# Routed experts of a decoder layer: the next block's transposes stand ahead of the up product, and streamed weights land in 14 places instead of 10

## The chip, the cores and the metric

The kernel runs on one core of one Trainium2 chip. The metric is the device time of one execution in microseconds, as the median of several runs. Besides, one execution was profiled by the hardware; durations of single instructions come from that one.

## The reference

One decoder layer works on 4096 tokens (2 sequences of 2048) of width 512, in float32. Three parts follow each other, each added to its input: an attention whose keys and values are fixed weights, with squared ReLU in place of the softmax; a cross-attention of 16 heads onto 128 context rows; and a mixture of experts. The last part is what the change is about, cut to its core:

```
shared = (silu(x @ sg) * (x @ su)) @ sd                  # every token, inner width 1024
e      = argmax(x @ gate_w);  xs = x * sigmoid(max(x @ gate_w))
for each expert r of 32, on the tokens with e == r:
    h      = silu(xs @ rg[r]) * (xs @ ru[r])              # 512 -> 1024
    routed = h @ rd[r]                                    # 1024 -> 512
out = x_in + shared + routed
```

Each expert has three matrices of 2 MB (gate, up, down), so the 32 experts read 201 MB of weights once.

## The kernel before, in words

TensorE works in float32r, a rounded format, so every float32 operand is split into a high part (a rounding copy) and a low part (the difference). A product takes three matmuls, low x high, high x low and high x high (`three`, L162). The high part is made by ScalarE (L93) and the low part by VectorE or POOL (L96), in `split`. In the profile the parts are named with h and l at the end: rh and rl of weights, th and tl of transposed inputs, hh and hl of hidden values.

The stages are `stage0` (attention), `stage1` (cross-attention, and the router's logits), `shared` with the first 768 of the shared expert's 1024 inner columns, and `routed`, which holds the experts and the last 256 inner columns of the shared expert (class `Rest`, L798). An `overflow` loop at the end takes tokens that didn't fit; here it runs no turn.

**The routed stage.** Experts are ranked by their number of tokens, and each rank has a fixed capacity (L30): 448, 384, five of 256, four of 192, thirteen of 128, eight of 64. A capacity is cut into blocks of 256, 128 or 64 rows. The order (L862 to L869, L1023 to L1033) mixes them: a large expert, then one of 64, then one of 128, and after each expert that isn't of 128 a block of the rest (256 tokens of the shared expert's remainder), until the sixteen of those are used. So a typical round is 256, rest, 64, rest, 128; the last rounds are 192 (128 + 64), 128, 128 without any rest.

The loop over the blocks (L1079 to L1100) is a pipeline written out by hand. For block i it emits:
- `prepare` (L1036) of block i+2: the indirect gather of its rows on POOL's queue (L905), or the rest's four z loads on SyncE's queue (L812),
- `load` of the next expert's gate weights, if this is the expert's last block,
- `first`: the gate product of block i (L941 for up to 128 rows; L986, with half of gate and up together, for 256; L823 for the rest),
- `load` of the next expert's up weights,
- `turn_hidden` of block i-1: its hidden values are transposed by TensorE (L912, `ht`) and split into th and tl,
- `second`: the up product of block i, after which VectorE or POOL multiplies it into the gate's silu,
- `turn_x` of block i+1: its gathered rows are transposed by TensorE (L912 or L931, `pt`) and split,
- `third`: the down product of block i-1 (L941, L1011 or L852), the copy out of PSUM (L1017, L855), and POOL's transfer that adds it into the output (L1019, L856),
- `load` of the next expert's down weights.

**Weights.** `load` (L882) takes eight pieces of 128 x 512 (256 KB) of one matrix. Each lands by SyncE's queue (L893) in a raw place, is cast by ScalarE into rh and gets its rl from VectorE; then the place is free. There are ten raw places: six of the pool `raw` (L55) and four of the tag F (L48). L872 says in which order they are taken. The split pieces of gate and up lie in a pool W of 48, of which the rest's weights hold some; those of down in the tags A and B, eight each.

**Other places.** Transposed inputs have two places each for th (tag J) and tl (tag K). A block of up to 128 rows takes one of each, a block of 256 both. Gathered rows have three (H). [...] P1 for the down product and for `pt` of up to 128 rows, P2 for gate, P3 for up, P4 for `ht` and for `pt` of 256 rows. The tag F serves earlier stages too: a low part in `stage0` and `stage1`, and the second half of the input tiles z of every other turn of `shared`.

**What sets the order.** The loop gives the instructions priorities in the order of emission. When the program is built, a scheduler places them on each engine's queue, by those priorities and its own estimate of when operands are ready; so casts of weights and casts of inputs are interleaved on ScalarE. On the chip each queue runs in that fixed order. An instruction that waits holds all that stand behind it on its engine.

## Time and profile before

| | us |
|---|---|
| median of 3 runs | 2779.28 (2778.81 to 2779.35) |
| the profiled execution | 2778.45 |
| its span, first to last instruction | 2776.4 |
| granted TensorE clock over the span | 0.993 of full speed |

| stretch of the span, us | what runs | TensorE busy | DMA, GB/s |
|---|---|---|---|
| 800 to 1000 | cross-attention | 195.81 of 200 | 69 |
| 1600 to 1700 | shared expert | 100.00 of 100 | 85 |
| 2000 to 2100 | routed experts | 98.11 of 100 | 275 |
| 2600 to 2700 | routed experts, last rounds | 96.46 of 100 | 305 |

How to read the lines that follow: the first number of a timeline line is the start in us from the span's begin, the second the time in us; then come the engine, the line of the kernel, the operation, and output <- inputs. In brackets stands how long the engine had been idle and what ended that. A busy share of TensorE counts overlapping matmuls, and the end of a matmul is modelled: a 512-column matmul is shown with 0.39 us, but in an unbroken row one starts every 0.227 us. In a table of stretches the columns are the stretch, its length, the busy us of TensorE, its weight loads, VectorE, ScalarE and POOL (with numbers of instructions), the granted TensorE clock, the busy share of the DMA engines and GB/s.

### The profile page before, as it was taken

Reading aid. Unit: us, or ns where it says so; the run is one execution under the profiler, and the core shown is the slowest. Engines: PE = TensorE matmul, PEld = TensorE weight load, DVE = VectorE, ACT = ScalarE, POOL = GpSimd, SP = SyncE. Lnnn points to the kernel's source line nnn. Section 1 sums busy time; section 2 is a strip of 40 time slices with the busy share of each in tenths; the row PEclk is TensorE's granted clock in tenths of the full one; section 3 lists DMA queues with packets and bytes.
Section 4 is the critical chain, followed back from the end, with each engine's and each line's share of the span. In section 5 each row is a group of like instructions: output and inputs, shape, how many; then the busy total and the mean of one; then the engine's idle time right before and its main releaser. Section 6 shows DMA issues by size and latency. Waiting matters only on the chain. (4 is left out here: it accounts for less than half of the span.)

```text
span 2776.4 us, 47492 instructions
## 1 busy us (share of the span) xinstructions
PE 2694.0 (97%) x14788; PEld 2298.8 (83%) x14788; DVE 2054.5 (74%) x4671; ACT 1793.1 (65%) x3995; POOL 1023.1 (37%) x821
## 2 busy tenths in 40 slices
PE   7999999999999999999999999999999999999997
PEld 5877877777878999899988888888888988877876
DVE  8888888889887988888878522245677777777885
ACT  6787777787867777777774111135566666667774
POOL 5686566677643333333330120002122222223232
PEclk9999999999999999999999999999999999999999
DMA  4022212212120223222245322255798989988984
GB/s 139 31 69 73 73 54 77 72 50 76 36 81 25 86 78 115 86 93 74 81 155 183 103 92 87 91 175 165 250 284 269 285 257 292 280 276 254 307 300 144
DMA packets 238001, 396.70 MB, mean 143 GB/s; under 512 B 29377, under 2 KB 67281, under 8 KB 237745
## 3 DMA queue, kind: packets, MB, share of 16 engines
q1 hardware_dynamic: 223024, 366.45, 39.2%
q0 software_dynamic: 14720, 27.19, 5.1%
q8 instruction: 117, 1.92, 0.3%
q14 instruction: 140, 1.14, 0.1%
HBM read 311.67 MB, written 83.83 MB: 142 GB/s over the span
## 5 line engine op out<-in xcount | busy, mean ns | idle before, releaser
L96 DVE TENSOR_TENSOR rl<-raw,rh 128x512 fp32r<-128x512 f32 x768 | 512.1, 711 | 124.1 <-ACT rh L93 116.6
L93 ACT CAST rh<-raw 128x512 fp32r<-128x512 f32 x768 | 446.3, 621 | 146.3 <-DMA raw<-in_rg 85.1
L96 POOL TENSOR_TENSOR pl<-p,ph 128x512 fp32r<-128x512 f32 x320 | 427.9, 1346 | 243.2 <-ACT ph L93 217.7
L343 DVE TENSOR_TENSOR p<-s,rl 128x512 f32<-128x512 f32 x512 | 343.2, 683 | 80.7 <-ACT rl L341 60.4
L93 ACT CAST ph<-p 128x512 fp32r<-128x512 f32 x448 | 277.3, 622 | 153.9 <-DVE p L343 148.4
L341 ACT ACTIVATE rl<-s 128x512 f32<-128x512 f32 x512 | 301.5, 599 | 34.5 <-PE s L337 20.7
L1019 POOL DMA_INDIRECT out_dram<-v,idx x46 | 92.5, 2010 | 407.1 <-ACT v L1017 277.4
L448 ACT ACTIVATE e<-e,nm 128x128 f32<-128x128 f32 x512 | 199.2, 391 | 63.1 <-DVE nm L445 62.7
L451 POOL TENSOR_TENSOR e<-e,ri 128x512 f32<-128x512 f32 x128 | 133.4, 1043 | 238.5 <-DVE ri L449 121.2
L298 PE MATMUL o<-pl,vwh 128*128 128x512 f32 x512 | 207.6, 405 | 11.1 <-DVE pl L96 7.5
L337 PE MATMUL s<-qh,kwl 128*128 128x512 f32 x512 | 207.1, 406 | 8.3 <-DVE p L343 8.1
L337 PE MATMUL s<-ql,kwh 128*128 128x512 f32 x512 | 200.6, 392 | 0.0
L337 PE MATMUL s<-qh,kwh 128*128 128x512 f32 x512 | 200.5, 392 | 0.0
L298 PE MATMUL o<-ph,vwh 128*128 128x512 f32 x512 | 200.0, 391 | 0.0
L298 PE MATMUL o<-ph,vwl 128*128 128x512 f32 x512 | 198.6, 392 | 0.0
L96 DVE TENSOR_TENSOR pl<-p,ph 128x512 fp32r<-128x512 f32 x192 | 184.4, 961 | 16.3 <-ACT ph L93 15.0
L905 POOL DMA_INDIRECT x<-xs,idx x46 | 53.0, 1152 | 356.1 <-DMA raw<-in_ru 167.4
L422 PE MATMUL q<-yh,wql 128*128 128x256 f32 x512 | 149.3, 292 | 2.8 <-DVE v L481 2.6
L93 ACT CAST hh<-s 128x512 fp32r<-128x512 f32 x92 | 57.1, 620 | 146.7 <-DVE s L760 118.9
L422 PE MATMUL q<-yh,wqh 128*128 128x256 f32 x512 | 145.4, 284 | 0.0
L422 PE MATMUL q<-yl,wqh 128*128 128x256 f32 x512 | 144.8, 283 | 0.0
L755 PE MATMUL u<-z,sw 128*128 128x512 f32 x576 | 139.9, 390 | 0.0
(296 smaller groups left out, 7640.3 us busy)
## 6 DMA issues: line engine op xcount, KB each, us to landing
raw<-in_rg SPq DMA_DIRECT2D x256, 256.0 KB, 5.3
raw<-in_ru SPq DMA_DIRECT2D x256, 256.0 KB, 6.0
raw<-in_rd SPq DMA_DIRECT2D x256, 256.0 KB, 4.4
z<-zT SPq DMA_DIRECT2D x128, 256.0 KB, 5.1
b<-x SPq DMA_DIRECT2D x64, 256.0 KB, 2.6
xt<-in_x SPq DMA_DIRECT2D x32, 256.0 KB, 2.7
x<-xt SPq DMA_DIRECT2D x32, 256.0 KB, 2.0
x<-b SPq DMA_DIRECT2D x32, 256.0 KB, 2.1
```

What stands on the lines that cost most here:

```text
L93: g.nc.scalar.copy(hi, src)
L96: (lo_engine or g.nc.vector).tensor_tensor(lo, src, f32(hi), A.subtract)
L298: nc.tensor.matmul(o[:], w, y[:], start=kt == 0 and n == 0, stop=kt == 15 and n == 2)
L337: nc.tensor.matmul(s[:], w, y[:], start=n == 0, stop=n == 2)
L341: m0 = nc.scalar.activation(r[:], s[:], AF.Relu)
L343: m1 = nc.vector.tensor_tensor(p[:], s[:], r[:], A.mult)
L422: nc.tensor.matmul(o[:, i, :], part(w, k, p), y[k // 2][:, k % 2, :], start=n == 0, stop=n == 11)
L448: nc.scalar.activation(e[:, hs], e[:, hs], AF.Exp, bias=nm[:, h:h + 1], scale=0.125, accum_out=su[:, h:h + 1])
L451: nc.gpsimd.tensor_tensor(e4, e4, ri[:].unsqueeze(2).to_broadcast([128, 4, 128]), A.mult)
L755: nc.tensor.matmul(p[:], part(w, k, c), y[k][:], start=n == 0, stop=n == 11)
L905: nc.gpsimd.indirect_dma_start(out=x[rows], out_offset=None, in_=xs, in_offset=bass.IndirectOffsetOnAxis(ap=idx[rows, b + j:b + j + 1], ax ...
L1019: nc.gpsimd.indirect_dma_start(out=out, out_offset=bass.IndirectOffsetOnAxis(ap=idx[rows, b + j:b + j + 1], axis=0), in_=v[rows], in_offse ...
```

## The change

Three things. `turn_x` of the next block is emitted right after `first`, ahead of `turn_hidden`, and `load` of the up weights after both, so both stand ahead of `second`. The tag F gets eight places instead of four, and the order in which raw places are taken is a new cycle of fourteen, six of the pool and eight of F. [...]

```diff
-    SLOTS = {"A": 8, "B": 8, "C": 5, "D": 4, "E": 4, "F": 4, "G": 4, "H": 3, "I": 2, "J": 2, "K": 2}
+    SLOTS = {"A": 8, "B": 8, "C": 5, "D": 4, "E": 4, "F": 8, "G": 4, "H": 3, "I": 2, "J": 2, "K": 2}
...
-    turns = {"u": cycle("W"), "d": cycle("A" * 8 + "B" * 8), "raw": cycle("rrFrrFrrFF")}
+    turns = {"u": cycle("W"), "d": cycle("A" * 8 + "B" * 8), "raw": cycle("rFrFFrFrFFrFrF")}
...
         first(*block)
+        if i + 1 < len(blocks):
+            turn_x(*blocks[i + 1])
+        if i > 0:
+            turn_hidden(*blocks[i - 1])
         if last and r in nxt:
             load(nxt[r], "u")
-        if i > 0:
-            turn_hidden(*blocks[i - 1])
         second(*block)
-        if i + 1 < len(blocks):
-            turn_x(*blocks[i + 1])
         if i > 0:
             third(*blocks[i - 1])
...
-    nc = bacc.Bacc("TRN2", target_bir_lowering=False, num_devices=1)
+    nc = bacc.Bacc("TRN2", target_bir_lowering=False, num_devices=1, dynamic_dma_scratch_size=8192)
```

## The prediction, made before the changed kernel ran

> **What bounds the kernel now.** I read the busy shares and slices first. They put TensorE at 97% of the span and show one stretch, from slice 28 on, where DMA is at 8 or 9 tenths as well. That stretch is the routed stage, the only place that the edit to the loop touches.

> ```profile
> PE 2694.0 (97%) x14788; PEld 2298.8 (83%) x14788; DVE 2054.5 (74%) x4671; ACT 1793.1 (65%) x3995; POOL 1023.1 (37%) x821
> ...
> DMA  4022212212120223222245322255798989988984
> ```

> TensorE is the bound, so a change can save only what TensorE loses. The stage's own table over 1850 to 2764 us gives 889.47 us busy of 914.00, so 24.5 us stand idle. The waits of TensorE from 1850 us to the end say for what (the columns are the sum in us, the times, the longest):

> ```profile
> PE g L986 <- ACT th L93: 6.7, 6, 3.0
> PE g L941 <- ACT th L93: 5.9, 2, 3.9
> PE d L941 <- ACT th L93: 4.1, 2, 3.1
> PE u L986 <- DVE rl L96: 2.9, 4, 1.2
> PE d L941 <- DVE th L96: 1.6, 2, 1.1
> PE pt L912 <- DVE b L776: 1.4, 1, 1.4
> ```

> The first two lines are gate products of the next block that wait for its transposed input. Why is that input late? ScalarE's timeline around the 3.0 us case shows it:

> ```profile
> 2227.37 1.14 ACT L93 CAST rh<-raw 128x512 fp32r<-128x512 f32 x2
> 2229.18 1.83 ACT L93 CAST rh<-raw 128x512 fp32r<-128x512 f32 x3 [0.68 <-DMA raw<-in_ru]
> 2232.12 0.62 ACT L93 CAST rh<-raw 128x512 fp32r<-128x512 f32 x1 [1.11 <-DMA raw<-in_ru]
> 2233.74 0.62 ACT L93 CAST rh<-raw 128x512 fp32r<-128x512 f32 x1 [1.00 <-DMA raw<-in_ru]
> 2234.26 0.58 ACT L93 CAST th<-pt 128x512 fp32r<-128x512 f32 x1
> ```

> The transposes were done at 2227.7, but their cast stands in ScalarE's order behind seven casts of weights, and three of those wait for a transfer, 0.68 + 1.11 + 1.00 = 2.79 us in all. TensorE waited 3.01 us, to 2234.89. So late weights hold an input that has nothing to do with them. SyncE's own waits from 1850 us say why the weights are late; the table of stretches beside it shows a lull and the stall:

> ```profile
> SPq L893 <- DVE rl L96: 335.8, 274, 48.8
> ```

> ```profile
> 2189.00:2193.00 4.00, 4.00 (x19) 3.33 (x18) 1.97 (x4) 3.06 (x6) 1.60 (x1) 1.00 0.29 74
> ...
> 2233.00:2237.00 4.00, 2.11 (x10) 2.11 (x11) 2.96 (x5) 3.26 (x7) 0.85 (x1) 0.61 1.04 399
> ```

> Weight loads wait 335.8 us for a place that VectorE has to free. Counted from issues and ends of the low parts, 8 to 10 of the 10 places are taken at every look between 2150 and 2246 us. At 2189 us they are full of landed data and DMA falls to 0.29 busy and 74 GB/s; at 2233 us it runs flat out at 399 GB/s and is late.

> The last row shows a second loss: the granted clock, the third column from the end, is 0.61. A shorter stall does the same:

> ```profile
> 2322.60:2326.00 3.40, 3.40 (x18) 3.40 (x18) 3.09 (x6) 3.28 (x7) 1.42 (x2) 0.50 1.04 385
> ```

> Just before it TensorE had stood 1.20 us (at 2320.0) and 0.75 us (at 2322.0). Over seven stretches of 100 us from 2000 to 2700 the granted clock reads 0.98, 1.00, 0.97, 0.98, 0.97, 0.98, 0.98: 14 us lost in seven halved phases.

> **The ceiling.** 24.5 us idle and, outside the idle time, about 13 us of clock: 37 us. Of these 1.4 us (the first block) and about 2 us (the last down product, after which only the drain follows) are not touched. So at most 34 us can go, plus noise.

> **The change, part by part.** The sum is made against the profiled execution, 2778.45 us (span 2776.4 and 2.05 around it), which stands 0.8 us under the median of the runs.

> *The transposes move.* No instruction is added or removed: per routed block four to eight transposes (109 ns apart at 128 columns, so 0.45 to 0.9 us), one or two casts on ScalarE (0.58) and the low parts on VectorE (0.68). In the built order of the changed kernel they stand just ahead of the up product. That gives the input the up product as extra cover: 24 x 0.227 = 5.4 us for a 128-row block, 16 x 0.227 = 3.6 for 64 rows, 24 x 0.12 = 2.9 for the shared rest. The 3.9 us stall at 2493.6 (transposes at 2486.4, cast at 2492.9) is covered by 5.4 us, and so is the other one of that line. It takes away 5.9 us. The gathered rows are there: from issue of a gather to its first transpose I count at least 22 us, and 6.4 us is the median landing; so no new wait on POOL, where the gathers can only go out sooner. The P1 bank for the transposes is freed by the copy of an earlier down product; where that is tightest (the 128-row block after a rest) the copy has the second half of that product and a rest gate product, 1.4 + 2.9 us, and costs 0.58. I take nothing for it.

> For a 256-row block the second half of the input can't be cast earlier, since it takes the place (J, K have two) of the running block's input, free only after the up product. There only the weights help.

> *Fourteen places.* No instruction changes, only when SyncE may issue. Four more transfers of 256 KB are 1.05 MB, 3.0 us at 350 GB/s, which fit into lulls like the one at 2189. In the case above ScalarE's 2.79 us of waiting would go and the cast would start at 2231.5, ending when TensorE asks (2231.9): 0.2 us left of 3.01. I take 5.2 of the 6.7 us, and 2.0 of the 2.9 us of late low parts. What is late next there is the up weight of the 256-row expert: its first low part is ready 0.05 to 1.2 us before its use in each of these rounds, so some of it stays.

> The weights stage in SP's queue too: z loads of the rest (four, each waiting for a release; 34.2 us of SyncE's waits) now stand behind all eight gate loads in place of two. In the round shown they were issued at 2182.9 for a use at 2205.0, and the six gate loads took 9.7 us, so some 12 us are left. I take nothing.

> *Hidden transposes.* Now the next input's cast stands ahead of the two hidden casts, 0.6 us on ScalarE and 0.7 on VectorE, up to 1.3 us. Where the current block is the rest, the cover to the down product is only 2.9 us, and in the trace two of eight such places already stall (1.1 us at 2535.8). Against that, weights that are earlier unblock the same queue. Bounds: 4 us gained, 10 lost (eight places at 1.3). The rows of the down waits, 6.6 us with 2 of them at the end, stand nearest to no change: zero.

> *The clock.* [...] The row at 2322.6 has 0.50 after waits of 1.20 and 0.75 us, so I count all seven phases. I take five as gone, one of them twice as long as the others: about 9 us. [...]

> *The scratch* for POOL's transfers is halved to make room. [...] the trace never has more than a few in flight. Zero.

> Sum: 5.9 + 5.2 + 2.0 + 0 + 9 = 22 us, so 2756.4 beside 2778.45, or 2757 beside the median. About 0.2% (5.6 us) is what a measurement can tell from no change.

> **The rivals.**
> - *DMA is the bound.* [...] then places only move the waiting. For it: 0.88 to 0.93 busy in the stretches of 100 us. Against it: 278 GB/s there, 399 at the peak, 74 in the lull. Only the moved transposes then pay: 5.9 and the clock of two phases, 3: 2770. Chance 0.15.
> - *Nearly all stalls go,* down waits too, since they hang on the same late weights: 33 us, 2746. Chance 0.2.
> - *Nothing measurable:* the next wait takes over each time. 2778. Chance 0.07.
> - *Slower.* With its input ready, the next gate product stands ahead of part or all of the down product in TensorE's built order, and the three casts stand together late in ScalarE's. In the last 260 us, where no rest is left and VectorE is 0.8 busy, the down product loses its old cover (10 us where a gate product lay between) and keeps 3.6 to 5.4. It decides if the casts come over 5 us after the transposes, as at 2658 to 2665.5. Twelve such blocks at 1.5 us and 1 us of clock are 30 us, less 22 gained: 2787. Chance 0.08. Against it: the gate weights there are ready 6 us or more before their use.
> - The forecast, 2757: 0.5.

> Faster 0.85, same 0.07, slower 0.08. The range leaves out the slower case and the ends of the others: 2743 (the ceiling) to 2775.

> **What would show it.** The waits of the gate products on th near 1 us; SyncE waiting less for places; no DMA slice like the 0.29; PEclk at 0.99 or 1.00 from 2000 to 2700; down waits near 6 us. It is wrong if down waits on th grow over 10 us, or if ScalarE's 85 us of waiting for gate transfers stay with the clock still halved each round.

## The result, and the profile after

| | before | after |
|---|---|---|
| median, us | 2779.32 (4 runs, 2778.81 to 2787.37) | 2744.56 (4 runs, 2742.13 to 2748.00) |
| the profiled execution | 2778.45 | 2744.97 |
| its span | 2776.4 | 2743.2 |
| granted clock over the span | 0.993 | 0.997 |

The ratio is 0.9882, with an interval from 0.9856 to 0.9907 (the two medians alone give 0.9875). The change makes the kernel faster by 34.8 us, 33.2 us in the two spans. The forecast was 22 us. 2744.56 lies inside its range, 1.6 us above the lower end, and next to the rival "nearly all stalls go", 2746. So the range held because it reached down to the ceiling, not because the sum was right.

Where in the span did it happen? TensorE's first product of the routed stage starts at 1844.0 us before and at 1847.0 after, its last matmul at 2763.7 and 2732.6. So the stage took 919.7 us and takes 885.6: 34.1 less. The earlier stages got 3.0 us longer, and the drain after the last matmul fell from 12.7 to 10.6 us. I don't explain the drain: e3 below, whose instructions stand in the order of before on every engine, has 10.5.

The waits of TensorE in the kernel after, from 1850 us to the end (sum in us, times, longest). These are all that reach 0.4 us:

```profile
PE d L941 <- ACT th L93: 1.0, 1, 1.0
PE g L941 <- ACT th L93: 0.9, 1, 0.9
PE g L941 <- DVE th L96: 0.7, 2, 0.4
PE g L986 <- DVE tl L96: 0.7, 1, 0.7
PE g L986 <- ACT th L93: 0.6, 2, 0.3
PE d L941 <- DVE tl L96: 0.4, 1, 0.4
```

The two gate lines with 6.7 and 5.9 us are down to 0.6 and 0.9, the down line from 4.1 to 1.0, and the line of late low parts (2.9) is gone. In all 24.5 us idle became 4.5. The remaining 1.0 of the down product is the one at the very end. How far do such sums vary by themselves? e3 runs the instructions of before and shows 29.8 us in place of 24.5, e9 those of the change and shows 3.1 in place of 4.5; a single line moves by up to 2 us.

Then the stretches of 2000 to 2700 and of the lull, after:

```profile
2000.00:2700.00 700.00, 697.64 (x3981) 607.27 (x3980) 557.37 (x885) 510.47 (x958) 189.44 (x117) 1.00 0.92 293
2189.00:2193.00 4.00, 4.00 (x20) 3.30 (x19) 4.00 (x7) 3.71 (x7) 1.36 (x1) 1.00 0.59 93
```

Before, the first of them read 679.49 busy, a clock of 0.98, a DMA share of 0.90 and 280 GB/s, and the second a DMA share of 0.29. The clock's part of the gain is what the waits leave: 34.1 less 20.0, some 14 us. The halved phases give the same: 27.3 us at half clock before, which is 13.7 us lost, and none after in this stage. DMA, which one rival took to be at its limit, moved 293 GB/s in place of 280.

ScalarE's timeline, after, around the input cast that came at 2234.26 before:

```profile
2225.20 0.58 ACT L93 CAST th<-pt 128x512 fp32r<-128x512 f32 x1
2225.67 3.75 ACT L93 CAST rh<-raw 128x512 fp32r<-128x512 f32 x7
2229.32 0.59 ACT L93 CAST th<-pt 128x512 fp32r<-128x512 f32 x1
```

This is the mechanism in three lines. The input's second half (a 256-row block) still stands behind seven casts of weights, as before. But they now run without a break, 0.54 us apart, and no bracket shows a wait for a transfer: each weight lay in its place. TensorE's line behind it shows what is left of the 3.01 us, 0.27:

```profile
2229.96 0.39 PE L986 MATMUL g<-th,rl 128*128 128x256 f32 x1 [0.27 <-ACT th L93]
```

### The profile page after: what moved, and what is told of

The parts are those of the page before. It is cut to its first block, busy times and chain, and to the rows that moved or that the text cites. A ratio compares the mean times of both kernels' runs of the same rounds, so it can differ in the third digit from the quotient of the medians.

```text
span 2743.2 us, 47449 instructions
## 1 busy us (share of the span) xinstructions
PE 2681.9 (98%) x14788; PEld 2293.6 (84%) x14788; DVE 2054.2 (75%) x4671; ACT 1786.0 (65%) x3995; POOL 1033.7 (38%) x821
## 5 line engine op out<-in xcount | busy, mean ns | idle before, releaser
L96 DVE TENSOR_TENSOR rl<-raw,rh 128x512 fp32r<-128x512 f32 x768 | 510.5, 711 | 106.2 <-ACT rh L93 98.0
L93 ACT CAST rh<-raw 128x512 fp32r<-128x512 f32 x768 | 440.3, 622 | 135.7 <-DMA raw<-in_rg 82.8
L96 POOL TENSOR_TENSOR pl<-p,ph 128x512 fp32r<-128x512 f32 x320 | 427.4, 1344 | 242.9 <-ACT ph L93 219.0
L93 ACT CAST ph<-p 128x512 fp32r<-128x512 f32 x448 | 277.7, 622 | 153.9 <-DVE p L343 148.3
L1019 POOL DMA_INDIRECT out_dram<-v,idx x46 | 108.0, 2347 | 424.8 <-ACT v L1017 332.8
L96 DVE TENSOR_TENSOR pl<-p,ph 128x512 fp32r<-128x512 f32 x192 | 185.2, 965 | 16.1 <-ACT ph L93 13.7
L93 ACT CAST hh<-s 128x512 fp32r<-128x512 f32 x92 | 57.0, 620 | 164.3 <-DVE s L760 117.2
L755 PE MATMUL g<-z,sw 128*128 128x512 f32 x576 | 139.5, 390 | 1.7 <-ACT s L759 1.7
```

The lines of the kernel that those rows point to most:

```text
L93: g.nc.scalar.copy(hi, src)
L96: (lo_engine or g.nc.vector).tensor_tensor(lo, src, f32(hi), A.subtract)
L755: nc.tensor.matmul(p[:], part(w, k, c), y[k][:], start=n == 0, stop=n == 11)
L1019: nc.gpsimd.indirect_dma_start(out=out, out_offset=bass.IndirectOffsetOnAxis(ap=idx[rows, b + j:b + j + 1], axis=0), in_=v[rows], in_offse ...
```

## The experiments

Two theories stood against each other. A: late weights hold the inputs' casts in ScalarE's queue, so the four more places do most of it. B: the moved transposes do most of it, since the up product now covers the cast. Each experiment is given by its edit against before or against the changed kernel, in short form.

**Each part alone.** The changed loop with ten places and the old scratch (e1), and the old loop with fourteen places and the smaller scratch (e2).

```diff
# e1: the changed kernel, but
-    "F": 8 ... "raw": cycle("rFrFFrFrFFrFrF") ... dynamic_dma_scratch_size=8192
+    "F": 4 ... "raw": cycle("rrFrrFrrFF")
# e2: the changed kernel, but in the loop
-        turn_x(i + 1), turn_hidden(i - 1), load "u", second(i), third(i - 1)
+        load "u", turn_hidden(i - 1), second(i), turn_x(i + 1), third(i - 1)
```

> The changed order of the loop alone, with ten raw places and the old scratch. Theory A (weights that are late hold casts of inputs in ScalarE's queue, so the places carry most): about 2768 us; the gate waits of blocks up to 128 rows go (5.9 us) with the clock of two phases, while the waits of 256-row blocks on th (6.7) and on low parts (2.9) stay. Theory B (the cover of the up product carries most, the places little): about 2752, with the waits of 256-row blocks gone too and the clock at 1.00 from 2000 to 2700 us.

> Fourteen raw places and the smaller scratch alone, with the old order of the loop. Theory A: about 2752 us; waits on th fall below 4 us in all, the halved clock phases from six rounds to one or two. Theory B: about 2770; the gate waits of blocks up to 128 rows (5.9 us) stay as they are.

e1 took 2767.61 us (2761.44 to 2770.39) beside 2781.48 before on that chip, 0.9945 (0.9927 to 0.9964). e2 took 2750.38 (2747.90 to 2751.28), 0.9882 (0.9862 to 0.9901). A said 2768 and 2752, B 2752 and 2770. So places alone give some 31 us, moved transposes alone 14. Together they give 35, not 45: the parts overlap. The waits of TensorE in e1, over the same stretch, show which are left without places (the four longest sums, of 18.6 us in all):

```profile
PE g L986 <- ACT th L93: 6.4, 5, 1.9
PE d L941 <- ACT th L93: 3.7, 3, 2.2
PE g L941 <- DVE th L96: 2.7, 2, 2.3
PE g L941 <- ACT th L93: 1.9, 3, 1.4
```

The move did what it was meant to at the two gate products of up to 128 rows (L941) that had stalled, for 3.93 and 1.96 us: 0.21 and nothing are left there. But stalls of 2.27 and 1.38 us came up at other blocks of that line, so that its two rows fall only from 6.1 to 4.6. ScalarE shows the first of them:

```profile
2523.30 0.62 ACT L93 CAST rh<-raw 128x512 fp32r<-128x512 f32 x1 [3.85 <-DMA raw<-in_rg]
```

The input's cast is the next on ScalarE. Its transposes stood at 2518.74, ahead of an up product of 3.13 us, and the weight in the queue came later than that. For blocks of 256 rows the move did nothing that shows (L986, 6.7 to 6.4): their second half has no place to be cast into earlier. The down waits (4.1 to 3.7) came to stand at other blocks. With places alone, e2 (the main rows):

```profile
PE d L852 <- DVE b L776: 2.4, 1, 2.4
PE g L941 <- ACT th L93: 1.6, 5, 0.5
PE d L941 <- ACT th L93: 1.0, 1, 1.0
PE pt L912 <- DVE b L776: 0.7, 1, 0.7
```

Here the 256-row line is gone, the down wait has the 1.0 of the end only, and at the two old stalls of L941 0.17 and 0.26 us are left. The L776 waits are at the entry to the stage: transposes and a down product wait for VectorE's last sums of the shared stage (L776). All runs with the old loop and full transfers wait there (1.2 to 3.1 us), none with the changed loop does.

A fourth piece of the diff, the load of the up weights behind the hidden transposes, does nothing by itself: with that line alone moved, the program that is built has every engine's order as before. It wasn't run.

**The scratch alone** (e3): before, with `dynamic_dma_scratch_size=8192`, the third part of the change, which is there to make room for the four more places of F.

> [...] the built order is the same as before, instruction by instruction. Both theories: 2779 us, no difference. If POOL's transfers were held by the smaller scratch, its issue rows (2.0 us mean for the output, 1.15 for the gathers) would grow and the time with them, up to 2785.

2781.45 (2775.59 to 2790.42) beside 2781.48, 0.9998 (0.9985 to 1.0012). It costs nothing that shows. The zero of the forecast was an estimate; this run bears it out.

**Twelve places** (e6), the changed kernel with

```diff
-    "F": 8 ... "raw": cycle("rFrFFrFrFFrFrF")
+    "F": 6 ... "raw": cycle("rFrFrFrFrFrF")
```

> The changed kernel with 12 raw places (F has six). Theory A: half of what four places bring, 2754 us; some halved clock phases come back. Theory B: 2745, like the changed kernel.

2754.49 (2750.88 to 2756.36), 0.9898 (0.9878 to 0.9917): the gain of the four places comes in steps. Two more places bring 13 of the 23 us between e1 and the changed kernel.

**Is it the transfers' being late?** (e8) Before's order and its ten places, but each weight transfer brings only the first 256 of its 512 columns, which are then used twice. Half of each expert's matrices is left out, so the results are not the layer's.

```diff
-    nc.sync.dma_start(raw[:], m[rows * 128:(rows + 1) * 128, cols * 512:(cols + 1) * 512])
-    split(g, hi[k], lo[k], raw[:])
+    nc.sync.dma_start(raw[:, 0:256], m[rows * 128:(rows + 1) * 128, cols * 512:cols * 512 + 256])
+    twice = raw[:, 0:256].unsqueeze(1).to_broadcast([128, 2, 256])
+    split(g, *(v.rearrange("p (a n) -> p a n", a=2) for v in (hi[k], lo[k])), twice)
```

> The kernel before, order and ten places as they were, but each weight transfer brings only the first 256 of its 512 columns and the split reads them twice: half of each expert matrix is left out, while casts, low parts and matmuls stay. If transfers that come late are what holds ScalarE's queue (theory A): waits on th and low parts in the routed stage fall below 5 us and the time is 2745 or less, with no change to the loop. If the waits come from the place of the transposes in the order (theory B): 12 us of gate waits stay and the time is 2765 or more.

2750.81 (2748.56 to 2754.38), 0.9877 (0.9851 to 0.9903). That is nearer to A (2745 or less) than to B (2765 or more), but not A whole. Its longest sum of waits and its stretch (line numbers from L894 on are one higher):

```profile
PE g L942 <- ACT th L93: 4.0, 7, 1.1
```

```profile
2000.00:2700.00 700.00, 695.04 (x3951) 602.78 (x3950) 547.54 (x874) 502.96 (x944) 176.30 (x116) 1.00 0.64 169
```

With DMA at 0.64 busy the gate waits for a 256-row block are gone, the clock reads 1.00 over the stretch (one halved phase is left, at 2530), and 4.0 us of gate waits (L942) are left in seven pieces of at most 1.1 us. So late transfers had made the long stalls. The short ones have two causes. At five of the seven, ScalarE's cast of the input stands behind a cast that waited 5.8 to 6.1 us for a gate transfer, which came late even with half the bytes; I can't say why. At the other two (0.59 and 1.12 us) it stands behind casts of weights that had landed, so there the order alone is the cause. One row warns against a wrong indicator: ScalarE in e8 (sum in us, times, longest).

```profile
ACT rh L93 <- DMA raw<-in_rg: 84.4, 34, 7.6
```

It waits 84.4 us for gate transfers, with half the bytes as with all (85.1), and 82.8 after the change. So this sum doesn't tell whether TensorE loses anything; a wait with an input's cast behind it does. The sum for the up weights, those of the case at 2234, does follow the stalls. Before and after:

```profile
ACT rh L93 <- DMA raw<-in_ru: 18.3, 28, 2.0
```

```profile
ACT rh L93 <- DMA raw<-in_ru: 1.6, 2, 1.4
```

It is 13.3 us in e1, 1.3 in e2 and 2.8 in e8.

**More places, and which ones** (e5, e7). Sixteen by tag F, and fourteen made of eight of the pool `raw` and six of F. Both keep the changed loop.

```diff
# e5
+    "F": 10 ... "raw": cycle("rFrFFrFFrFFrFFrF") ... dynamic_dma_scratch_size=4096
# e7
+    name="raw", bufs=8 ... "F": 6 ... "raw": cycle("rrFrFrFrrFrFrF")
```

> The changed kernel with 16 raw places (F has ten, scratch 4096). With 14 places TensorE waits only 4.5 us from 1850 us on and the clock isn't halved in the routed stage, so late weights have nothing more to give: 2743 us, within 3. If the places still limit (each two having given 5 to 10 us from 10 to 12 to 14), it would be 2737 or less.

> The changed kernel with its 14 raw places as eight of the pool raw and six of F. The first rest product starts at 1847.0 us in the changed kernel and at 1847.4 with 14 places alone, but at 1844.0 to 1844.8 in every kernel whose F has four or six; so I expect the start near 1844.5, the routed stage as in the changed kernel, and 2742 us, 2.5 us less. If the later start has nothing to do with F's eight places, it stays at 1847 and the time at 2744.6.

e5 took 2737.93 (2736.58 to 2741.34) beside 2786.26 on that chip, 0.9832 (0.9806 to 0.9857). My number was 2743, for the case that the waits had no more to give; the other case, 2737 or less, came nearer. e7 took 2751.62 (2750.86 to 2755.95), 0.9884 (0.9862 to 0.9905), where 2742 was expected. It was to heal what F's eight places do at the start of the shared stage, shown by TensorE's stretch there, before and after:

```profile
1440.00:1480.00 40.00, 40.00 (x200) 33.20 (x199) 29.57 (x69) 28.61 (x52) 4.97 (x4) 1.00 0.75 259
```

```profile
1440.00:1480.00 40.00, 38.34 (x190) 31.33 (x189) 27.47 (x69) 26.76 (x49) 6.37 (x6) 1.00 0.73 246
```

The 1.66 us are one wait, at 1446. F holds tiles of that stage too, and the built order there changed. With eight places in F the wait is there in each profile (1.3 to 1.7 us); with four, six or ten at most 0.3 us of waiting shows in that stretch. In e7 it is gone, and the routed stage takes as long as with the change (885.5 us beside 885.6). But the pool `raw` serves the attention too: its last matmul stands at 820.7 us in place of 813.2. A buffer shared between stages moves all of them.

**The changed kernel, sixteen places and sixteen with the old loop, on one chip** (e9, e10, e11).

> The changed kernel once more, to have it beside 16 places on one chip: ratio 0.988 to the kernel before, TensorE waiting 4 to 5 us from 1850 us on, first rest product at 1847 us.

> The changed loop with 16 places once more, beside the changed kernel. Its routed stage ran from 1845.4 to 2726.2 in the profile, 4.8 us shorter than with 14, and it began 1.6 us earlier. If that is the places' doing, it is 5 to 7 us faster than the changed kernel here too (ratio 0.985 to 0.986); if the larger distance of the other call came from its chip, the two are within 2 us.

> 16 places with the old order of the loop. Theory A in its strong form (the moved transposes give nothing once the weights aren't late): within 2 us of 16 places with the new order. If the cover of the up product is worth something of its own, as 14 places with and without it suggest (2744.6 against 2750.4): 4 to 7 us slower than with the new order, with gate waits on th of 1 to 2 us left.

Beside 2780.14 before: the changed kernel 2745.04 (2741.94 to 2746.84), ratio 0.9879 (0.9860 to 0.9899); sixteen places 2737.06 (2735.67 to 2738.39), 0.9849 (0.9827 to 0.9870); sixteen with the old loop 2740.65 (2739.18 to 2742.40), 0.9860 (0.9839 to 0.9882). Sixteen places beat both kernels: no run of the changed kernel is as short as the longest of theirs. The move of the transposes is worth 14 us with ten places and 3.6 with sixteen, each on one chip. With fourteen it is some 5 to 6 (2750.4 to 2744.6 or 2745.0), but these medians come from different chips, and the ratios to before, 0.9882 and 0.9882 or 0.9879, don't tell the two apart. The profiles say where it lies. e2's routed stage takes 890.3 us, 4.6 and 6.2 more than the two with the changed loop; 3.1 of that are the waits at the entry and 1.7 a halved phase right behind them. With sixteen, 3.2 of 4.7 us in e11 lie there. So beside many places the move pays mostly at the entry to the stage, and little in the rounds that it was meant for. The waits of TensorE with sixteen places, e10:

```profile
PE d L941 <- ACT th L93: 1.0, 1, 1.0
PE d L941 <- DVE tl L96: 0.4, 1, 0.4
PE g L986 <- ACT th L93: 0.4, 1, 0.4
PE ht L912 <- POOL s L969: 0.3, 1, 0.3
```

With the changed loop, 10, 12, 14 and 16 places take 2767.6, 2754.5, 2744.6 and 2737.1 us: 13, 10 and 7.5 us for each two more. (The kernel before took 2779.3 to 2781.5 on these chips.) What stays open is part of the last step. In two profiles each, the routed stage takes 885.6 and 884.0 us with fourteen places, 880.8 and 880.7 with sixteen: 4.1 of the 7.5 us, of which the waits (4.5 and 3.1 to 2.3 and 2.1) are about 1.6. The drain gives 0.9 more (10.6 to 9.9 and 9.6). Some 2 us come from comparing medians with single executions: of the runs of e9 the profiled one is the fastest, of those of e10 the slowest. The other 2.5 us of the stage I can't place.

## Why the prediction was right, and where its sizes were wrong

The direction and the mechanism held: late weights kept inputs waiting in ScalarE's queue. The shares did not: the places alone give 31 of the 35 us, where the forecast gave the moved transposes 5.9 of its 13 us of waits. Term by term, over the routed stage:

| term | forecast, us | measured, us |
|---|---|---|
| gate products, up to 128 rows (of 5.9) | 5.9 | 4.3: waits of 0.9 + 0.7 are left |
| gate products, 256 rows (of 6.7) | 5.2 | 5.4: 0.6 + 0.7 left |
| late low parts (of 2.9) | 2.0 | 2.9 |
| down products and hidden transposes (of 6.6) | 0 | 5.2: 1.0 + 0.4 left |
| other short waits (of 2.4) | none | 2.2: 0.2 left; 1.4 of it is the first block's, which the ceiling had left out |
| clock | 9 | some 14 |
| **routed stage** | **22** | **34** |
| earlier stages | none | -3.0 |

- *The step that failed is the zero for the down products.* I named the bounds, 4 gained to 10 lost, and took the nearest row to be "no change", since the input's cast now stands ahead of the hidden casts. The longest of these waits, 3.08 us at 2666.16, was of the same kind as the gate stalls, hidden casts behind late weights, as ScalarE's timeline of before shows:

```profile
2664.88 0.62 ACT L93 CAST rh<-raw 128x512 fp32r<-128x512 f32 x1 [1.19 <-DMA raw<-in_ru]
2665.53 1.08 ACT L93 CAST th<-ht 128x512 fp32r<-128x512 f32 x2
```

e1 keeps 3.7 of the 4.1 us, e2 only the 1.0 at the end. So the places took them. The rival "nearly all stalls go" had said it: "since they hang on the same late weights". The three casts in one place in the queue cost nothing that can be seen in the changed kernel. With ten places (e1) one down product did wait 2.19 us, at 2509.63.
- *The clock was mis-sized by 5 us.* I took five of seven halved phases as gone, and all seven went: over 2000 to 2700 the clock reads 1.00 in each stretch of 100 us. The row with 0.50 after waits of 1.20 and 0.75 us was the right witness: phases after short waits count as well. How far the profiles show what decides is in the last section. e6 shows how near it is to coming back: with twelve places two halved phases are there again, at 2526.7 and 2642.7.
- *The 5.9 us put down to the moved transposes* would mostly have gone without them: e2 leaves 1.6 at that line, e1 leaves 4.6 of 6.1. At the two stalls that I had counted, either part alone is enough; against late weights elsewhere, the cover of an up product is not. The size was nearly right, and the cause was mostly the other part.
- *The 0.2 us forecast for the stall at 2235* measured 0.27, at 2229.96.
- *Early stages:* I followed the tag F only into the routed stage, though it serves others. The wait at 1446 costs 1.66 us, and two halved phases in the attention stages, which before doesn't have (the last section), 3.4. Together they make 5.1, where the routed stage begins 3.0 us later, and in e9, the same kernel, 1.5. So 2 to 3.5 us came back in those stages; by what, I didn't follow.
- *Rivals.* "DMA is the bound" fell by its own row: where it had read 264 and 305 GB/s (2500 to 2600, 2600 to 2700), the kernel after shows

```profile
2500.00:2600.00 100.00, 99.70 (x500) 82.73 (x499) 92.09 (x147) 81.71 (x158) 33.77 (x19) 1.00 0.95 308
2600.00:2700.00 100.00, 99.09 (x472) 81.58 (x471) 88.91 (x146) 80.17 (x152) 30.38 (x13) 1.00 0.93 313
```

so 0.84 to 0.93 busy hadn't been a limit (the prediction's 0.88 passes over the 0.84 of 2500 to 2600). "Slower" fell in the same rows: in the last 260 us, VectorE at 0.9 busy and no rest left, TensorE stands under 1 us in each 100, and the down product's 1.0 at the end is the wait that was there before.
- *Signs that I gave and that misled.* SyncE's waiting for places should have fallen and hardly did, 335.8 to 320.4 us: as I read it, the queue runs further ahead with more places and still waits for one, only earlier. DMA's lulls should have gone; of the 175 stretches of 4 us from 2000 to 2700, 15 before and 11 after are under 0.5 busy. TensorE's waits went all the same. And ScalarE's 85 us of waiting for gate transfers stayed (82.8) while the stalls went; its waiting for up transfers, 18.3 to 1.6, was the sum to name. The surest sign is the wait just ahead of an input's cast.

## What to carry to other kernels

When a resource waits in an in-order queue, look at what stands ahead of it and why that is late: here an input's cast stood behind seven casts of weights, and TensorE waited 3.01 us in before and 0.27 after. More landing places for a stream can free work that isn't part of the stream, even with DMA at 0.90 busy (2000 to 2700 in before; the places alone gave 31 us). Two edits that treat the same stall don't add up (14 and 31 us gave 35), so each is to be timed alone; and a place that is borrowed from another stage must be followed into that stage.

## What the hardware showed that was not expected

In these profiles TensorE's clock is at 0.50 for 3.41 us after some short waits (0.95 and 2.04 us in the changed kernel), and the length of one wait doesn't say after which. In before and after the same wait of 2.04 us stands in the cross-attention, before first:

```profile
841.69 0.66 PE L464 MATMUL pt<-ident,e 128*128 128x128 f32 x4 [2.04 <-DVE pl L96]
```

```profile
841.22 0.94 PE L464 MATMUL pt<-ident,e 128*128 128x128 f32 x4 [2.04 <-DVE pl L96]
```

```profile
837.80:841.21 3.41, 1.84 (x14) 1.42 (x13) 1.14 (x3) 3.38 (x15) 2.28 (x3) 1.00 0.04 10
841.21:844.62 3.41, 2.71 (x18) 2.26 (x19) 2.65 (x6) 3.16 (x9) 1.04 (x1) 1.00 0.00 0
```

and of the changed kernel:

```profile
838.05:841.46 3.41, 1.37 (x10) 0.94 (x10) 1.42 (x4) 3.38 (x15) 1.57 (x2) 1.00 0.01 3
841.46:844.87 3.41, 3.41 (x18) 3.36 (x17) 2.59 (x6) 2.60 (x7) 1.04 (x1) 0.50 0.00 0
```

The last column but two is the granted clock. In the changed kernel the whole wait falls into one stretch of the grid, TensorE is busy for 1.37 of its 3.41 us, and the next stretch runs at 0.50. In before the grid cuts the wait, TensorE is busy for 1.84 us, and the clock stays. All twelve profiles agree at this wait: the seven whose stretch has at most half of it busy halve the clock, the five with 0.54 or more (before, e1, e3, e6, e8) don't.

The same holds over all some 9500 stretches of the grid in these profiles, from where the clock's record begins (some 22 us into before and after). Every one with TensorE busy for less than 0.43 of it is followed by a halved phase; none with more than 0.59 is, but for a stretch that was itself halved. In between both occur, and the ends of matmuls are modelled, so the limit isn't known more closely. Of the seven phases of the kernel before, only one follows a stretch without any work; the others follow 0.28 to 0.58 busy. In line with this, a halved phase follows 1.20 and 0.75 us, most of them within one stretch (0.54 busy), at 2322.6, and none follows 1.12 us alone in a stretch (0.67 busy) at 2535.8.

The grid lies differently against the work in each execution: at this wait it begins at 837.8 in before and 837.6 in e3, at 838.0 in after and 838.4 in e9. So the two halved phases of the changed kernel need not be its doing. This is read from the profiles; no run was made to test it.
